# The engine that signals the entry of a kernel's main section: GpSimd in place of SyncE

## The chip, the cores and the metric

The kernel runs on one core of a Trainium2 chip. The metric is the time on the device of one execution, in microseconds (us). The core has a matrix engine (TensorE, PE in the profile, with PEld for its weight loads), VectorE (DVE), ScalarE (ACT), GpSimd (POOL) and SyncE (SP). Each has a sequencer of its own that works through its own list of instructions; the engines meet only through semaphores. A sequencer's own work (waits, branches, DMA issues) is shown with a q behind the engine's name. The transfers issued by SyncE and ScalarE run on the same 16 DMA engines; in the profile, SyncE's are queue q1 and ScalarE's are queue q10.

## The reference

For each of 128 samples b, a matrix of 128 by 128 is picked from eight by the sample's subject, and its product with the sample is added to the sample:

```python
x: (128, 128, 1024) float32; itok_B_0_7: (128,) int32; L0_cond_weights: (8, 128, 128) float32
w = weights[subjects]
out = jnp.einsum('bct,bcd->bdt', x, w)
x = x + out
```

So 67.1 MB of x are read and 67.1 MB written, beside 0.5 MB of matrices.

## The kernel before

The 128 samples are worked on in 32 turns of four samples (two halves, h, of two samples each). `x_all` holds 12 slots of one turn each in the core's memory; the sum is formed in place, so that a slot is loaded, added to, stored from, and loaded again.

Nearly all of the kernel is one section, opened at L190 with `tc.tile_critical()`. Within it nothing is ordered for the author: each engine's list is written out by hand, with semaphores. The lists are these.

- SyncE: the load of the eight matrices (L192) into the last slot's room, the load of the subjects (L195), and then, in the loop of L247, a wait for `s_added` and a store for each turn (the first one at L251, the others through `transfer`, L67), in pairs of turns towards the end.
- ScalarE: the loads of x, four transfers a turn, 128 in all, through `transfer` (L67). From turn 12 on a turn waits until its slot has been stored; turn 11, whose slot holds the raw matrices at first, waits until they have been sorted (`s_sort`).
- VectorE: the zeros (L197), the sorting of the matrices (two transposes, L208 and L227, and copies, L230), the clamping of the subjects (L211 to L217), and then in a loop of 32 turns (L263) the sum of a half (L186) and the two matrices of the next (L165).
- GpSimd: four of the sorting copies (L230), then for each turn a wait until its loads have landed, which it passes on to TensorE as `s_ready` (L242 to L245).
- TensorE: six passes over zeros while nothing has arrived (L200), then in a loop (L268) eight matrix products a turn (L174), each half after `s_go` (its matrices are in place) and `s_ready`.

Ahead of the section the program opens with a barrier of all engines, in which GpSimd gathers the others and then releases them; in the profile it stands under L297 (GpSimd also writes four constants there). At the section's entry one engine, the signalling engine, raises a semaphore with a NOP, and every engine, itself included, waits for it on the branch that leads into the section. The NOP stands under L190, the branches under L306. Where the section ends, the signalling engine raises another semaphore, all five engines drain, the signalling engine gathers the five and raises a semaphore with a second NOP; these stand under L190 too.

Behind the section comes a second, short one (L272), in which ScalarE waits for the stores that are still under way, and the last store (L275), of 4 MB, which SyncE issues once the first section has ended. The program ends with the wait for that store and two barriers (L306).

Of the kernel before, what the change touches and what calls it, by code (L numbers as in the profile page):

```python
# [80 lines left out]
def kernel(  # L81
# [48 lines left out]
    def emptied(i):  # L130
        turns = i // SLOTS
        return DMA * (H * G + 1) * turns - (DMA * G if i >= SLOTS and i % SLOTS == 0 else 0)

    def load(engine, i, q):
        transfer(
            nc,
            engine,
            xs[i % SLOTS][:, q, :],
            x[i * H * G + q].rearrange("(a r) t -> a (r t)", r=ROWS),
        ).then_inc(s_head if i * H * G + q < G else s_slot[i % SLOTS], DMA)  # L140

    def store(i, n):
        at = i % SLOTS * H * G * T
        return transfer(
            nc,
            nc.sync,
            out[i * H * G : (i + n) * H * G].rearrange("g d t -> d g t"),
            x_all[:, at : at + n * H * G * T].rearrange(
                "d (o t) -> d o t", o=1 if i >= NT - WHOLE else n
            ),  # L150
        )

    def subjects_of(i):
        _, subject = nc.values_load_multi_w_load_instructions(
            index[0:1, i] if isinstance(i, slice) else index[0:1, bass.ds(i * (H * G), H * G)],
            engines=[mybir.EngineType.DVE],
            min_val=0,
            max_val=S - 1,
            skip_runtime_bounds_check_because="the index is clamped on the chip above",
        )  # L160
        return subject

    def place(h, subject):
        for q in range(h * G, (h + 1) * G):
            copy = nc.vector.tensor_copy(ws[q], w_all[:, bass.ds(subject[q], 1), :])  # L165
        copy.then_inc(s_go, 1)

    def multiply(slot, h):
        nc.tensor.wait_ge(s_go, 1).then_inc(s_go, -1)
        nc.tensor.wait_ge(s_ready, 1).then_inc(s_ready, -1)  # L170
        for q in range(h * G, (h + 1) * G):
            for t in range(0, T, N):
                at = slot * (H * G * T) + (q * T + t)
                mm = nc.tensor.matmul(  # L174
                    ps[h][:, q % G, t : t + N],
                    ws[q][:, 0, :],
                    x_all[:, bass.ds(at, N)],
                    start=True,
                    stop=True,
                )  # L180
        mm.then_inc(s_product, 1)

    def add(slot, h):
        mine = x_all[:, bass.ds(slot * (H * G * T) + h * G * T, G * T)]
        nc.vector.wait_ge(s_product, 1).then_inc(s_product, -1)  # L185
        nc.vector.tensor_tensor(  # L186
            mine, ps[h].rearrange("d g t -> d (g t)"), mine, ALU.add
        ).then_inc(s_added, 1)

    with tc.tile_critical():  # L190

        nc.sync.dma_start(  # L192
            w_raw, weights.rearrange("s (u j) d -> (s u) (j d)", j=S)
        ).then_inc(s_wall, DMA)
        nc.sync.dma_start(given, subjects.rearrange("(o b) -> o b", o=1)).then_inc(s_given, DMA)  # L195

        nc.vector.memset(zeros, 0.0).then_inc(s_zeros, 1)  # L197
        nc.tensor.wait_ge(s_zeros, 1)
        for _ in range(IDLE):
            nc.tensor.matmul(  # L200
                ps[P_SLOTS - 1][:, G - 1, :N], zeros[:, :D], zeros, start=True, stop=True
            )

        nc.vector.wait_ge(s_wall, DMA)
        nc.vector.transpose(  # L208
            w_mid.rearrange("p (e h w j) -> p j h e w", e=S, h=4, w=4), w_raw
        ).then_inc(s_sort, 1)  # L210
        nc.vector.memset(index[:, B:], 0).then_inc(s_index, 1)  # L211
        nc.vector.wait_ge(s_given, DMA)
        nc.vector.tensor_scalar(near, given, -S, S - 1, ALU.max, ALU.min).then_inc(s_index, 1)  # L213
        nc.vector.wait_ge(s_index, 2)
        nc.vector.tensor_scalar(wrap, near, 0, S, ALU.is_lt, ALU.mult).then_inc(s_index, 1)  # L215
        nc.vector.wait_ge(s_index, 3)
        nc.vector.tensor_tensor(index[:, :B], near, wrap, ALU.add).then_inc(s_index, 1)  # L217
        for i in range(NT):
            if i == SLOTS - 1:
                nc.scalar.wait_ge(s_sort, SORTED)  # L220
            if i >= SLOTS:
                nc.scalar.wait_ge(s_slot[i % SLOTS], emptied(i))
            for q in range(H * G):
                load(nc.scalar, i, q)

        nc.vector.wait_ge(s_sort, 1)
        nc.vector.transpose(w_late, w_mid).then_inc(s_sort, 1)  # L227

        def sort(engine, o, v):
            engine.tensor_copy(  # L230
                w_all[32 * v : 32 * (v + 1), 2 * o : 2 * (o + 1), :],
                w_late[32 * o : 32 * (o + 1)].rearrange("c (e v d) -> c v e d", v=4, d=D)[:, v],
            ).then_inc(s_sort, 1)

        nc.vector.wait_ge(s_sort, 2)
        nc.gpsimd.wait_ge(s_sort, 2)
        for o in range(4):
            for v in range(4):
                sort(nc.gpsimd if v == 3 else nc.vector, o, v)
        for i in range(NT):  # L240
            if i == 0:
                nc.gpsimd.wait_ge(s_head, DMA * G).then_inc(s_ready, 1)  # L242
                nc.gpsimd.wait_ge(s_slot[0], DMA * G).then_inc(s_ready, 1)
            else:
                nc.gpsimd.wait_ge(s_slot[i % SLOTS], emptied(i) + DMA * H * G).then_inc(s_ready, H)  # L245

        for i in [*range(NT - SLOTS), *range(NT - SLOTS, NT, PAIR)]:  # L247
            n = 1 if i < NT - SLOTS else PAIR
            nc.sync.wait_ge(s_added, (i + n + (BEHIND if EARLY <= i < NT - LAST else 0)) * H)
            if i == 0:  # L250
                nc.sync.dma_start(  # L251
                    out[: H * G].rearrange("g d t -> d g t"), xs[0]
                ).then_inc(s_slot[0], DMA)
            elif i + n < NT:
                store(i, n).then_inc(s_slot[i % SLOTS], DMA)


        nc.vector.wait_ge(s_index, 4)
        nc.vector.wait_ge(s_sort, SORTED)
        subject = subjects_of(slice(0, H * G))  # L260
        for h in range(H):
            place(h, subject)
        with nc.vector.Fori(0, NT) as turn:  # L263
            subject = subjects_of(turn + 1)
            for h in range(H):
                add(turn % SLOTS, h)
                place(h, subject)
        with nc.tensor.Fori(0, NT) as turn:  # L268
            for h in range(H):
                multiply(turn % SLOTS, h)  # L270
# [39 lines left out]
```

## Time and profile before

| | |
|---|---|
| median of 3 runs | 323.01 us (322.72, 323.01, 323.01) |
| profiled execution, time | 322.73 us |
| profiled execution, span from first to last instruction | 320.9 us |
| TensorE busy | 248.9 us (78%), 518 matmuls |
| VectorE busy | 172.6 us (54%), 216 instructions |
| GpSimd busy | 1.9 us (1%), 8 instructions |
| moved by DMA | 134.76 MB, 420 GB/s over the span |

The span is the profile's own time axis, and all moments are counted from its start. The time of an execution is 1.8 us longer than its span. An engine's busy time leaves out what only its sequencer does. In a row of the view by line, the three numbers are the shortest, median and longest duration in ns, and the next two are the first and the last start in us; an instruction is listed when any part of it lies in the stretch asked for.

### The profile page before, as it was taken

Reading aid. Unit: us, or ns where it says so; the run is one execution under the profiler, and the core shown is the slowest. Engines: PE = TensorE matmul, PEld = TensorE weight load, DVE = VectorE, ACT = ScalarE, POOL = GpSimd, SP = SyncE. Lnnn points to the kernel's source line nnn. Section 1 sums busy time; section 2 is a strip of 40 time slices with the busy share of each in tenths; the row PEclk is TensorE's granted clock in tenths of the full one; section 3 lists DMA queues with packets and bytes.
Section 4 is the critical chain, followed back from the end, with each engine's and each line's share of the span. In section 5 each row is a group of like instructions: output and inputs, shape, how many; then the busy total and the mean of one; then the engine's idle time right before and its main releaser. Section 6 shows DMA issues by size and latency. Waiting matters only on the chain. (4 is left out here: it accounts for less than half of the span.)

```text
span 320.9 us, 2386 instructions
## 1 busy us (share of the span) xinstructions
PE 248.9 (78%) x518; PEld 102.8 (32%) x518; DVE 172.6 (54%) x216; POOL 1.9 (1%) x8
## 2 busy tenths in 40 slices
PE   6199999999997699998498469988599957874000
PEld 2134444444433244443133224333244422331000
DVE  4636776777676167775435362675367745066000
POOL 0200000000000000000000000000000000000000
PEclk9679999999999599999789797999799989599555
DMA  7999999999999999999999999999999999999996
GB/s 294 425 425 412 426 423 432 429 423 425 425 425 425 425 424 425 425 429 425 429 435 431 427 427 429 425 425 425 425 425 425 425 425 425 427 427 455 429 445 274
DMA packets 10803, 134.76 MB, mean 420 GB/s; under 512 B 2481, under 2 KB 2482, under 8 KB 3122
## 3 DMA queue, kind: packets, MB, share of 16 engines
q1 hardware_dynamic: 4658, 67.64, 49.7%
q10 hardware_dynamic: 6144, 67.12, 49.6%
q14 instruction: 1, 0.01, 0.0%
HBM read 67.63 MB, written 67.11 MB: 420 GB/s over the span
## 5 line engine op out<-in xcount | busy, mean ns | idle before, releaser
L174 PE MATMUL ps<-x_all,w 128*128 x512 | 243.8, 635 | 42.0 <-PEq L170 34.3
L186 DVE TENSOR_TENSOR x_all<-ps,x_all 128x2048 f32 x64 | 146.7, 2292 | 117.3 <-DVEq L185 117.3
L174 PEld LDWEIGHTS ps<-x_all,w 128*128 128x128 f32 x512 | 100.9, 203 | 185.2 <-issue 184.6
L165 DVE COPY w<-w_all 128x128 f32 x132 | 23.2, 219 | 0.8 <-DVE w_all L230 0.8
L200 PE MATMUL ps<-zeros 128*128 128x512 f32 x6 | 5.2, 1033 | 1.7 <-DVE zeros L197 1.7
L230 DVE COPY w_all<-x_all 32x256 f32<-32x256 f32 x12 | 3.9, 326 | 0.4
L208 DVE STREAM_TRANSPOSE x_all<-x_all 128x1024 f32<-128x1024 f32 x1 | 2.0, 1992 | 3.1 <-DMA x_all<-in_L_cond_weights_dram 3.1
L200 PEld LDWEIGHTS ps<-zeros 128*128 128x128 f32 x6 | 1.8, 328 | 3.7 <-issue 2.1
L230 POOL COPY w_all<-x_all 32x256 f32<-32x256 f32 x4 | 1.7, 425 | 8.3 <-DVE x_all L227 8.1
L227 DVE STREAM_TRANSPOSE x_all<-x_all 128x1024 f32<-128x1024 f32 x1 | 1.2, 1225 | 0.0
L197 DVE MEMSET zeros<- 128x512 f32 x1 | 0.5, 485 | 1.0 <-SPq L190 1.0
L217 DVE CUSTOM_DVE_ANT_0 index<-near,wrap 1x256 uint16<-1x256 uint16 x1 | 0.3, 280 | 0.0
L215 DVE TENSOR_SCALAR wrap<-near 1x128 int32<-1x128 int32 x1 | 0.2, 215 | 0.0
L213 DVE TENSOR_SCALAR near<-given 1x128 int32<-1x128 int32 x1 | 0.2, 205 | 0.0
L297 POOL MEMSET const-bfloat16-1.0<- 128x1 bf16 x1 | 0.1, 100 | 0.0
L297 POOL MEMSET const-float32-0.0<- 128x1 f32 x1 | 0.1, 98 | 0.2 <-issue 0.2
L297 POOL MEMSET const-uint8-127<- 128x1 uint8 x1 | 0.1, 98 | 0.0
L297 POOL MEMSET const-float32-1.0<- 128x1 f32 x1 | 0.1, 97 | 0.0
L297 DVE BASE_LOAD x1 | 0.0, 21 | 0.1
L211 DVE MEMSET index<- 1x4 int32 x1 | 0.1, 62 | 0.0
## 6 DMA issues: line engine op xcount, KB each, us to landing
x_all<-in_x_dram ACTq DMA_DIRECT2D x128, 512.0 KB, 34.2
out_dram<-x_all SPq DMA_DIRECT2D x20, 2048.0 KB, 18.3
out_dram<-x_all SPq DMA_DIRECT2D x6, 4096.0 KB, 30.3
x_all<-in_L_cond_weights_dram SPq DMA_DIRECT2D x1, 512.0 KB, 3.7
given<-in_itok_B_dram SPq DMA_DIRECT2D x1, 0.5 KB
```

Source lines behind the costliest of these rows:

```text
L165: copy = nc.vector.tensor_copy(ws[q], w_all[:, bass.ds(subject[q], 1), :])
L174: mm = nc.tensor.matmul(ps[h][:, q % G, t : t + N], ws[q][:, 0, :], x_all[:, bass.ds(at, N)], start=True, stop=True,)
L186: nc.vector.tensor_tensor(mine, ps[h].rearrange("d g t -> d (g t)"), mine, ALU.add).then_inc(s_added, 1)
L197: nc.vector.memset(zeros, 0.0).then_inc(s_zeros, 1)
L200: nc.tensor.matmul(ps[P_SLOTS - 1][:, G - 1, :N], zeros[:, :D], zeros, start=True, stop=True)
L208: nc.vector.transpose(w_mid.rearrange("p (e h w j) -> p j h e w", e=S, h=4, w=4), w_raw).then_inc(s_sort, 1)
L213: nc.vector.tensor_scalar(near, given, -S, S - 1, ALU.max, ALU.min).then_inc(s_index, 1)
L215: nc.vector.tensor_scalar(wrap, near, 0, S, ALU.is_lt, ALU.mult).then_inc(s_index, 1)
L217: nc.vector.tensor_tensor(index[:, :B], near, wrap, ALU.add).then_inc(s_index, 1)
L227: nc.vector.transpose(w_late, w_mid).then_inc(s_sort, 1)
L230: engine.tensor_copy(w_all[32 * v : 32 * (v + 1), 2 * o : 2 * (o + 1), :], w_late[32 * o : 32 * (o + 1)].rearrange("c (e v d) -> c v e d", ...
L297: nc = _bacc.Bacc("TRN2", target_bir_lowering=False, num_devices=1)
```

## The change

One argument is added. It names the engine that signals the entry and the end of the main section. Without it that engine is SyncE here.

```diff
-    with tc.tile_critical():
+    with tc.tile_critical(sync_engine=mybir.EngineType.Pool):
 
         nc.sync.dma_start(
             w_raw, weights.rearrange("s (u j) d -> (s u) (j d)", j=S)
```

No transfer, compute instruction, wait or size of the section itself is changed; the second section, at L272, keeps ScalarE as its signalling engine.

## The prediction

> **What bounds the kernel now.** I read the page first: the table of slices, the DMA queues, the total traffic.
>
> ```profile
> span 320.9 us, 2386 instructions
> ...
> DMA  7999999999999999999999999999999999999996
> ...
> q1 hardware_dynamic: 4658, 67.64, 49.7%
> q10 hardware_dynamic: 6144, 67.12, 49.6%
> ...
> HBM read 67.63 MB, written 67.11 MB: 420 GB/s over the span
> ```
>
> Only the first and last of 40 DMA slices are under 9, and both queues together fill 99.3% of the 16 engines. So I asked for the stretches at the two ends and between them (start:end us, length, four engines, granted clock, DMA share, GB/s).
>
> ```profile
> 1.50:2.01 0.51, 0.34 (x1) 0.34 (x2) 0.11 (x1) 0.00 (x0) 1.00 0.00 0
> 2.01:2.03 0.02, 0.02 (x1) 0.02 (x1) 0.00 (x0) 0.00 (x0) 1.00 6.40 410
> 2.03:6.00 3.97, 3.97 (x5) 1.48 (x5) 1.29 (x1) 0.00 (x0) 1.00 0.98 369
> 6.00:300.00 294.00, 244.60 (x514) 100.94 (x512) 170.82 (x214) 1.70 (x4) 0.92 1.01 427
> 300.00:317.50 17.50, 0.00 (x0) 0.00 (x0) 0.00 (x0) 0.00 (x0) 0.50 0.98 419
> ...
> 318.40:320.00 1.60, 0.00 (x0) 0.00 (x0) 0.00 (x0) 0.00 (x0) 0.50 0.01 0
> ```
>
> No byte starts before 2.01 us, none after 318.4, and between 6 and 300 us the engines move 427 GB/s at a share of 1.01. 134.76 MB (the page's two directions added) at 427 GB/s take 315.6 us; the stream stands from 2.01 to about 318.3. What can be won is at the ends: 2.0 us ahead of the first byte, about 2.6 us behind the last, and 1.8 us outside the span (the profiled execution took 322.73 us). PE and DVE may move by tenths without an effect as long as both queues are supplied. The end of the span is a wait for the last store, in the DMA queues' own waits:
>
> ```profile
> SPq L306 <- DMA out_dram<-x_all: 23.7, 1, 23.7
> ```
>
> Now the first two microseconds, in order of time:
>
> ```profile
> 0.34 0.10 POOL L297 MEMSET const-uint8-127<- 128x1 uint8 x1
> 0.90 1.18 ACTq L67 DMA_DIRECT2D x_all<-in_x_dram  x2
> 0.96 0.41 SPq L192 DMA_DIRECT2D x_all<-in_L_cond_weights_dram  x1
> 1.12 0.48 DVE L197 MEMSET zeros<- 128x512 f32 x1 [0.99 <-SPq L190]
> ```
>
> DVE's first work of the section is put down to SP's line 190, the entry of the section: this is the signal that the change takes from SyncE. The sequencers' own instructions appear in the view by line; one-decimal starts are too coarse, so I asked for stretches of hundredths. The rows below come from 0.605:0.615, 0.645:0.665 (two rows), 0.71:0.72, 0.75:0.765 (two rows) and 0.79:0.82 us:
>
> ```profile
> L297 POOLq EVENT_SEMAPHORE  x1: 17/17/17, 0.6 to 0.6; - x1
> ...
> L297 SPq EVENT_SEMAPHORE  x1: 17/17/17, 0.7 to 0.7; - x1
> L297 ACTq EVENT_SEMAPHORE  x1: 17/17/17, 0.7 to 0.7; - x1
> ...
> L190 SPq NOP  x1: 18/18/18, 0.7 to 0.7; - x1
> ...
> L306 ACTq COMPARE_BRANCH  x1: 33/33/33, 0.8 to 0.8; - x1
> L306 POOLq COMPARE_BRANCH  x1: 33/33/33, 0.8 to 0.8; - x1
> ...
> L306 SPq COMPARE_BRANCH  x1: 33/33/33, 0.8 to 0.8; - x1
> ```
>
> This is a ladder of two signals. GpSimd ends the program's opening barrier at 0.61 and the others see it at 0.655: a hop of 0.045. SyncE goes on to its NOP at 0.715 (0.06 after its event), which is the entry signal; ScalarE and GpSimd branch into the section at 0.757 (a hop of 0.042). SyncE, which has to pass its own NOP, branches only at 0.80. The first DMA issues follow, ScalarE's at 0.90 and SyncE's at 0.96: 0.14 to 0.16 behind their branches.
>
> **The change, part by part.** *Entry.* The NOP and its signal move from SyncE to GpSimd; no transfer and no compute instruction is added or removed. GpSimd raises the barrier itself, so it need not see it first: the SyncE hop goes. No row shows a NOP on GpSimd; I give it SyncE's step from barrier to NOP, 0.06, so it falls at 0.61 + 0.06 = 0.67, and a hop of 0.042 brings it to the others at 0.71. ScalarE and SyncE are themselves ready at 0.655 + 0.06 = 0.715; that is late next, so nothing better can come. ScalarE's branch moves from 0.757 to 0.715: -0.04. SyncE's moves from 0.80 to 0.715: -0.08. Behind the new wait on SyncE stand the loads of the matrices (L192) and of the subjects (L195); on ScalarE the loads of x; on DVE the zeros.
>
> Which of the two queues opens the stream? From 2.00 to 3.76 us the DMA view answers:
>
> ```profile
> DMA packets 108, 0.44 MB, mean 251 GB/s; under 512 B 0, under 2 KB 0, under 8 KB 108
> ...
> q1 hardware_dynamic: 108, 0.44, 86.7%
> ```
>
> Queue 1 alone, in small packets: the matrices, issued by SyncE. x, though issued 0.06 us earlier, has no packet before 3.76. So the start of the stream goes with SyncE's issue, and I take -0.08; if it went with ScalarE's it would be -0.04. The best end is -0.08. The worst uses the longest GpSimd sequencer row of the page's end that waits for nothing:
>
> ```profile
> L306 POOLq EVENT_SEMAPHORE_RANGE_CLEAR  x1: 201/201/201, 320.4 to 320.4; - x1
> ```
>
> A NOP that took 0.20 would signal at 0.87, seen at 0.91: +0.11 on SyncE and +0.15 on ScalarE. I stay near SyncE's NOP because GpSimd's EVENT_SEMAPHORE (17 ns) and COMPARE_BRANCH (33 ns) above take exactly what ScalarE's take.
>
> [...]
>
> *What the earlier start does.* The stream is full from 6 us on, so a start 0.08 earlier ends 0.08 earlier. Matrices that land 0.08 earlier let the sort and the first product start 0.08 earlier; that is worth nothing more, as DMA and not PE is full.
>
> *Exit.* The end of the section is signalled by the same engine, so it moves to GpSimd too. Now (295 to 296 us, then the closing wait of ScalarE, and GpSimd's waits for x):
>
> ```profile
> L190 SPq EVENT_SEMAPHORE  x3: 17/28/28, 295.3 to 295.5; - x3
> ...
> L190 POOLq DRAIN  x1: 41/41/41, 295.3 to 295.3; - x1
> L190 DVEq DRAIN  x1: 85/85/85, 295.3 to 295.3; - x1
> ...
> L190 SPq NOP  x1: 13/13/13, 295.6 to 295.6; - x1
> ...
> L306 ACTq EVENT_SEMAPHORE  x5: 38/38/14502, 295.7 to 310.5; - x5
> ...
> L245 POOLq EVENT_SEMAPHORE  x31: 17/17/17, 14.6 to 285.1; - x31
> ```
>
> SyncE signals the end, five engines drain, SyncE gathers them and goes on in its own program to the last store. With GpSimd gathering, the last store waits for one more hop, +0.04, and its gather may cost up to the 0.20 above. GpSimd is there in time: its last wait ends at 285.1, ten microseconds ahead. The cost is hidden: from 295.7 to the end the queue moves this much,
>
> ```profile
> q1 hardware_dynamic: 343, 9.67, 93.3%
> ...
> out_dram<-x_all SPq DMA_DIRECT2D x1, 4096.0 KB, 24.3
> ```
>
> of which 4.19 MB are the last store. The other 5.48 MB are stores queued ahead of it, 13 us at 419 GB/s, and ScalarE sees the last of those land only 14.5 us after 295.7. So 0.24 us of delay costs nothing; without that cover it would cost 0.24. Behind the last store SyncE has only the final wait.
>
> Sum: 322.73 - 0.08 (entry) + 0 (exit, hidden) = 322.65 for the profiled execution. That execution lies 0.28 below the median of the runs shown, 323.01, whose lowest is 322.72; from the median the forecast is 323.01 - 0.08 = **322.93**. A difference of 0.2% (0.65 us) is about what a measurement of this kernel can tell from no change, and 0.08 is an eighth of it: **no change that can be measured**.
>
> **The rivals.** *Nothing is gained, or GpSimd's NOP is slow.* If the NOP on GpSimd takes effect no earlier than 0.715, the start stays: 322.73, or 323.01 from the median. If it takes 0.20, the start slips by 0.11: 322.84, or 323.12. For it: no GpSimd NOP is in the trace. Also within 0.2%.
>
> *Slower: the engines' last packets.* The stream's end is uneven. In 318.23:318.40, and then in 318.35:319.30, the DMA view has
>
> ```profile
> q1 hardware_dynamic: 3, 0.10, 135.4%
> ...
> q1 hardware_dynamic: 13, 0.00, 0.8%
> ```
>
> Three last packets of 33 KB start when the other 13 engines are already finishing (13 packets without bytes). At 427/16 = 26.7 GB/s per engine one packet takes 1.23 us. If the shifted start changes how loads and stores alternate so that one engine falls a further packet behind, the end slips by 1.23: 322.65 + 1.23 = 323.88 (324.16 from the median), slower by 0.36%. It decides from half a packet on (0.65 us). Against it: every engine has the same bytes to move, and three runs of one program differ by only 0.29 us.
>
> *Faster: the same place, evened out.* The 0.10 MB spread over 16 engines take 0.23 us instead of 1.23: at best 1.0 us less, 321.65 (321.93). The same argument stands against it, and nothing in the change aims there.
>
> *Slower: x passes the matrices.* If x's first transfers reached the engines ahead of the matrices, each would delay them by 0.524 MB / 427 GB/s = 1.23 us, and sort, products and stores with them. The time grows only once the loads of the 12 slots (25.2 MB, 59 us at that rate, from 3.76 to 63) are through before the first store (the rows below: issued at 26.9, landed 23.8 later, at 50.7) has emptied a slot. That is 12 us of delay, or ten transfers passed; each further one costs 1.23: 322.65 + 1.23 = 323.88 for one. Against it: SyncE gains 0.04 on ScalarE by the change.
>
> ```profile
> L251 SPq DMA_DIRECT2D out_dram<-x_all x1: 424/424/424, 26.9 to 26.9; - x1
> ...
> DMA to landing us min/median/max: 23.8/23.8/23.8
> ```
>
> **How the numbers follow.** Forecast (entry 0.04 to 0.08 earlier) 0.70; nothing gained or a slow NOP 0.15; an engine a packet later 0.07; evened out 0.06; x ahead 0.02. The first two stay within 0.2%: same 0.85; slower 0.09; faster 0.06. The time is 322.93. The range takes the first two cases, which hold 0.85: from 322.93 less the runs' spread of 0.29, and 0.14 for a part of the even tail, 322.50; to 323.12 and, for a part of a later packet, 0.23: 323.35.
>
> **What would show it.** DVE's wait at L197 names GpSimd's queue at line 190, and the NOP of line 190 stands on GpSimd at 0.67. ScalarE's first issue is at 0.86 and SyncE's at 0.88; the first byte at 1.93 to 1.97; queue 1 alone until x starts at 3.7. The last store's issue stays within 0.2 us of 295.7 and its end at 318.2 to 319.6. I am wrong if the first byte comes later than 2.13, if DMA falls under 425 GB/s between 6 and 300 us, or if more or fewer than three packets are late at the end.

## The result, and the profile after

The changed kernel takes 323.73 us (median of 12 runs, 323.42 to 324.47), the kernel before 323.02 (12 runs, 322.72 to 323.61). The ratio is 1.0020, with a 95% interval of 1.0011 to 1.0029: slower by 0.7 us, where 322.93 and no measurable change were forecast. The range ended at 323.35.

The page of the changed kernel hardly differs, and the stretches (start:end, length, the four engines, granted clock, DMA share, GB/s) show the stream as full as before:

```profile
span 321.5 us, 2387 instructions
...
q1 hardware_dynamic: 4658, 67.64, 49.8%
q10 hardware_dynamic: 6144, 67.12, 49.5%
...
HBM read 67.63 MB, written 67.11 MB: 419 GB/s over the span
```

```profile
1.50:1.92 0.42, 0.25 (x1) 0.25 (x2) 0.11 (x1) 0.00 (x0) 1.00 0.00 0
1.92:1.94 0.02, 0.02 (x1) 0.02 (x2) 0.00 (x0) 0.00 (x0) 1.00 3.04 205
...
6.00:300.00 294.00, 239.93 (x513) 99.30 (x512) 170.97 (x214) 1.70 (x4) 0.93 1.01 427
300.00:317.50 17.50, 0.00 (x0) 0.00 (x0) 0.00 (x0) 0.00 (x0) 0.50 0.98 419
```

The rate between 6 and 300 us is the same 427 GB/s, and the first byte comes at 1.92 to 1.94 instead of 2.01 to 2.03: 0.09 earlier, close to the 0.08 that was forecast. The entry itself, first the order of time, then the view by line in stretches of hundredths (0.685:0.70, 0.725:0.735, 0.74:0.75 us):

```profile
0.89 1.18 ACTq L67 DMA_DIRECT2D x_all<-in_x_dram  x2
0.89 0.41 SPq L192 DMA_DIRECT2D x_all<-in_L_cond_weights_dram  x1
1.13 0.48 DVE L197 MEMSET zeros<- 128x512 f32 x1 [0.99 <-PEq L297]
```

```profile
L190 POOLq NOP  x1: 13/13/13, 0.7 to 0.7; - x1
...
L306 SPq COMPARE_BRANCH  x1: 33/33/33, 0.7 to 0.7; - x1
...
L306 ACTq COMPARE_BRANCH  x1: 33/33/33, 0.7 to 0.7; - x1
```

GpSimd's NOP stands at 0.69 and takes 13 ns. SyncE branches at 0.73 (0.80 before), ScalarE at 0.74 (0.757 before); their first issues now fall together.

So where are the 0.7 us? The profiled execution has a span of 321.5 and a time of 323.96: 2.46 us lie outside the span. Before it was 322.73 - 320.9 = 1.83. This holds for every run: the time less the span is 2.34 to 2.62 in the twelve runs of the changed kernel (median 2.47), and 1.73 to 1.84 in 132 runs of the kernel before that were made beside the experiments (median 1.78). The spans do not differ: on the mean 321.29 and 321.31. **All of the 0.7 us lies outside the span.** There, from 321 to 325 us (40 slices of 0.1 us), the DMA view of the changed kernel has one packet:

```profile
DMA  0000000000000000000000000000200000000000
GB/s 0 0 0 0 0 0 0 0 0 0 0 0 0 0 0 0 0 0 0 0 0 0 0 0 0 0 0 0 82 0 0 0 0 0 0 0 0 0 0 0
DMA packets 1, 0.01 MB, mean 2 GB/s; under 512 B 0, under 2 KB 0, under 8 KB 0
...
q14 instruction: 1, 0.01, 0.6%
```

and the same stretch of the kernel before has none:

```profile
DMA packets 0, 0.00 MB, mean 0 GB/s; under 512 B 0, under 2 KB 0, under 8 KB 0
```

It is a packet of instructions (82 GB/s for 0.1 us: 8.2 KB), at 323.8, which is 2.3 us behind the end of the span. My reading is that an engine fetches more of its list there; the view does not say which engine. The page does not tell the kernels apart in this: its count for q14 is 1 in both, for a packet that both profiles have between 116 and 117 us. The change moves instructions from one list to another: in the two programs GpSimd's list grows from 60 to 65 instructions, SyncE's shrinks from 49 to 45, the others stay. (The profiled executions agree in the differences: they hold 55 and 60 instructions of GpSimd, 45 and 41 of SyncE.)

### The profile page after: what moved, and what is told of

Its sections match the earlier page's. It is cut to its first block, busy times and chain, and to the rows that moved or that the text cites. A ratio compares the mean times of both kernels' runs of the same rounds, so it can differ in the third digit from the quotient of the medians.

```text
span 321.5 us, 2387 instructions
## 1 busy us (share of the span) xinstructions
PE 244.3 (76%) x518; PEld 101.1 (31%) x518; DVE 172.6 (54%) x216; POOL 1.9 (1%) x8
## 5 line engine op out<-in xcount | busy, mean ns | idle before, releaser
L174 PE MATMUL ps<-x_all,w 128*128 x512 | 239.6, 626 | 44.8 <-PEq L170 30.5
L174 PEld LDWEIGHTS ps<-x_all,w 128*128 128x128 f32 x512 | 99.3, 199 | 185.1 <-issue 184.5
L197 DVE MEMSET zeros<- 128x512 f32 x1 | 0.5, 485 | 1.0 <-PEq L297 1.0
L297 POOL MEMSET const-bfloat16-1.0<- 128x1 bf16 x1 | 0.1, 101 | 0.0
L297 POOL MEMSET const-float32-0.0<- 128x1 f32 x1 | 0.1, 98 | 0.2 <-issue 0.2
L297 POOL MEMSET const-float32-1.0<- 128x1 f32 x1 | 0.1, 98 | 0.0
L297 POOL MEMSET const-uint8-127<- 128x1 uint8 x1 | 0.1, 98 | 0.0
```

The source lines that it names most:

```text
L174: mm = nc.tensor.matmul(ps[h][:, q % G, t : t + N], ws[q][:, 0, :], x_all[:, bass.ds(at, N)], start=True, stop=True,)
L297: nc = _bacc.Bacc("TRN2", target_bir_lowering=False, num_devices=1)
```

## The experiments

Theory "outside": the price is the fetch, and hangs on the length of GpSimd's list. Rival "start": the two first issues now fall together, which lays the stream out worse. A later rival says that the cost comes of GpSimd's signalling, whatever the length of its list. `s_spare` in the edits is a semaphore that nobody waits for. Each kernel ran eleven times beside the kernel before; "outside" is the median of time less span.

**The kernel before again** (no edit).

> The kernel before, unchanged: it measures how far two equal programs differ, and how much of a time lies outside the span (the profiled execution before: 322.73 - 320.9 = 1.83 us; the changed kernel: 323.96 - 321.5 = 2.46, and 2.34 to 2.62 in all twelve of its executions). Theory 'outside the span' (the change costs its 0.6 us there): about 1.8 us outside, 323.0. Theory 'start' (the first issues of SyncE and ScalarE now fall together and the stream is laid out worse): nothing said of the outside; 323.0 and a span of 320.9 to 321.2. If about 2.4 us lies outside here too, the theory of the outside is dead.

Measured: 323.02, ratio 0.9998 (0.9989 to 1.0007), outside 1.78. Equal programs agree within the interval, and the outside belongs to the program.

**The changed kernel with SyncE's first issue later.**

```diff
     with tc.tile_critical(sync_engine=mybir.EngineType.Pool):
+        nc.sync.sem_inc(s_spare, 1)
         nc.sync.dma_start(
```

> The changed kernel with one semaphore increment more on SyncE ahead of the load of the matrices, some 0.06 to 0.08 us, which puts SyncE's first issue behind ScalarE's again (0.89 and 0.96 instead of 0.891 and 0.892). Theory 'start': back to 323.0, 0.7 under the changed kernel. Theory 'outside the span': stays at 323.7, as GpSimd still signals.

Measured: 323.79, ratio 1.0022 (1.0013 to 1.0031), outside 2.52. The issues are apart again, at 0.89 and 0.99:

```profile
0.89 0.53 ACTq L67 DMA_DIRECT2D x_all<-in_x_dram  x1
0.99 0.41 SPq L192 DMA_DIRECT2D x_all<-in_L_cond_weights_dram  x1
```

and nothing of the 0.7 us comes back. This speaks against "start".

**The kernel before with ScalarE's first issue later.**

```diff
+        nc.scalar.sem_inc(s_spare, 1)
...
         for i in range(NT):
             if i == SLOTS - 1:
```

> The kernel before with one semaphore increment more on ScalarE ahead of the loads of x, some 0.06 to 0.08 us, so that ScalarE's first issue falls together with SyncE's (0.97 and 0.96) while SyncE still signals. Theory 'start': 323.7, as slow as the changed kernel. Theory 'outside the span': 323.0.

Measured: 323.04, ratio 0.9999 (0.9990 to 1.0008), outside 1.79. The issues come within 0.02 of each other, at 0.95 and 0.97, and nothing is lost:

```profile
0.95 0.41 SPq L192 DMA_DIRECT2D x_all<-in_L_cond_weights_dram  x1
0.97 0.53 ACTq L67 DMA_DIRECT2D x_all<-in_x_dram  x1
```

Neither run bears "start" out, and the equal spans above speak against it too.

**The kernel before with GpSimd's list as long as in the changed kernel.**

```diff
                 nc.gpsimd.wait_ge(s_slot[i % SLOTS], emptied(i) + DMA * H * G).then_inc(s_ready, H)
+        nc.gpsimd.sem_inc(s_spare, 1); nc.gpsimd.sem_inc(s_spare, 1); nc.gpsimd.sem_inc(s_spare, 1); nc.gpsimd.sem_inc(s_spare, 1); nc.gpsimd.sem_inc(s_spare, 1)
```

> The kernel before with five semaphore increments more at the end of GpSimd's list in the section, which is then as long as in the changed kernel; they run at about 285 us, when nobody waits for GpSimd. Theory 'outside the span', if it is the length of GpSimd's list: 323.7 with 2.4 us outside the span. Theory 'start': 323.0.

Measured: 323.81, ratio 1.0020 (1.0011 to 1.0029), outside 2.52. SyncE signals, as before; five instructions that nobody waits for bring the whole loss, and the packet at the same place, 2.3 us behind a span of 321.1:

```profile
core 0 of [0], span 321.1 us
DMA  0000000000000000000000003000000000000000
...
DMA packets 1, 0.01 MB, mean 2 GB/s; under 512 B 0, under 2 KB 0, under 8 KB 0
...
q14 instruction: 1, 0.01, 0.8%
```

**Two instructions instead of five** (62).

```diff
+        nc.gpsimd.sem_inc(s_spare, 1); nc.gpsimd.sem_inc(s_spare, 1)
```

> The kernel before with two more semaphore increments at the end of GpSimd's list in the section (60 instructions become 62; 65 in the changed kernel). Theory 'a block of the list is fetched behind the span': the cost comes in one step of about 0.7 us at some length between 60 and 65, so either 323.0 with 1.78 us outside the span and no packet of instructions there, or 323.75 with 2.5 us and one packet. Rival 'each instruction on GpSimd costs': a part in proportion, 2/5 of 0.75 = 0.3, so 323.35.

Measured: 322.93, ratio 1.0001 (0.9992 to 1.0010), outside 1.80, no packet. So it is not a price per instruction.

**Another engine's list:** five increments on VectorE behind its loop (VectorE's list grows from 62 to 68).

```diff
                 place(h, subject)
+        for _ in range(5): nc.vector.sem_inc(s_spare, 1)
         with nc.tensor.Fori(0, NT) as turn:
```

> The kernel before with five more semaphore increments on VectorE behind its loop (and one register instruction that comes with them: 62 become 68, more than the 65 of GpSimd in the changed kernel). If any engine's list costs a fetch past some length, 323.75 with 2.5 us outside the span; if it is GpSimd's own matter, 323.0 and 1.78. The span itself stays at 321.3 by either, as the last store is far behind.

Measured: 323.11, ratio 1.0003 (0.9994 to 1.0012), outside 1.81. Neither branch of the expectation: there is a packet, but it costs 0.03. It comes earlier, in the slice at 322.3, 1.1 to 1.2 us behind the span of 321.2:

```profile
DMA  0000000000000200000000000000000000000000
```

**GpSimd's four sorting copies on VectorE**, in the changed kernel and, as control, in the kernel before (GpSimd 61 and 56, VectorE 66 in both).

```diff
-        nc.gpsimd.wait_ge(s_sort, 2)
...
-                sort(nc.gpsimd if v == 3 else nc.vector, o, v)
+                sort(nc.vector, o, v)
```

> The changed kernel, GpSimd still signals, but GpSimd's four sorting copies run on VectorE, which brings GpSimd's list down from 65 to 61 instructions and VectorE's up from 62 to 66. Theory 'the length of GpSimd's list': if the step lies above 61, 323.0 or a few hundredths less, 1.78 us outside the span, no packet of instructions behind it. Rival 'that GpSimd signals costs, whatever its length': 323.75 and 2.5. The sort is 1.3 us longer on VectorE, which the full DMA queues hide.

> The control for the run above: the kernel before, SyncE signals, with the four sorting copies on VectorE (GpSimd's list 56, VectorE's 66). By each theory 323.0, with 1.78 us outside the span and a span of 321.3; a difference from that is the price of the moved copies and is to be taken off the run above.

Measured: 323.34, ratio 1.0008 (0.9999 to 1.0017), outside 2.21; control 323.48, ratio 1.0017 (1.0008 to 1.0026), outside 2.19. The control, which should have cost nothing, costs as much: both profiles have a packet 1.7 us behind the span, and some 0.42 us more lie outside, whoever signals. I read it as a fetch of VectorE's longer list. Once that is taken off, GpSimd's signal costs nothing at 61; but the pair was a poor way to ask, as it moved two lists.

**The changed kernel with a shorter list**, nothing moved elsewhere (61).

```diff
+            elif i in (1, 3, 5, 7):
+                nc.gpsimd.wait_ge(s_slot[i], DMA * H * G)
             else:
-                nc.gpsimd.wait_ge(s_slot[i % SLOTS], emptied(i) + DMA * H * G).then_inc(s_ready, H)
+                nc.gpsimd.wait_ge(s_slot[i % SLOTS], emptied(i) + DMA * H * G).then_inc(s_ready, 2 * H if i in (2, 4, 6, 8) else H)
```

> The changed kernel, GpSimd signals, with GpSimd's list in the section cut from 65 to 61 instructions: turns 1 and 2, 3 and 4, 5 and 6, 7 and 8 are reported to TensorE by one instruction for two turns each; nothing moves to another engine. Theory 'the length of GpSimd's list': no packet of instructions behind the span, 1.78 us outside it, 323.0, or 322.95 if the entry's few hundredths show. Rival 'that GpSimd signals costs': 323.75, 2.5 us outside.

Measured: 322.92, ratio 0.9995 (0.9986 to 1.0004), outside 1.78, no packet. GpSimd signals, the two issues stand together at 0.89 as in the changed kernel, and the 0.7 us are gone:

```profile
core 0 of [0], span 321.2 us
...
DMA packets 0, 0.00 MB, mean 0 GB/s; under 512 B 0, under 2 KB 0, under 8 KB 0
```

This undoes the loss without undoing the change. It is no measurable gain over the kernel before.

**Four more on the kernel before (64), four and twelve more on the changed kernel (69 and 77)**: the same line, at the same place, with four, four and twelve increments.

> The kernel before with four more semaphore increments at the end of GpSimd's list (64 instructions; 62 cost nothing, 65 cost 0.7 us). Theory 'a block is fetched': one of the two levels, 323.0 with 1.78 us outside and no packet, or 323.75 with 2.5 us and one packet; nothing between.

> The changed kernel with four more semaphore increments on GpSimd (69 instructions instead of 65). Theory 'where the fetch falls sets its price': a longer list meets the end of its block earlier; VectorE's four more instructions put the fetch at 1.68 us behind the span for 0.42 us, two more still put it at 1.18 for 0.04. So here the fetch comes earlier than the 2.29 us of the changed kernel and costs less, 0.1 to 0.5: 2.0 to 2.3 us outside, 323.1 to 323.5. Rival 'a fetch costs 0.7, or more instructions cost more': 323.75 or above.

> The changed kernel with twelve more semaphore increments on GpSimd (77 instructions instead of 65). Theory 'where the fetch falls sets its price': the fetch comes earlier than 1.3 us behind the span, where GpSimd still has time before it is waited for: 0.0 to 0.1, so 1.78 to 1.9 us outside and 323.05, although the list is longer than in the changed kernel. Rival 'a fetch costs 0.7, or more instructions cost more': 323.75 or above.

Measured: 64: 323.29, ratio 1.0005 (0.9996 to 1.0014), outside 2.05, no packet in the profile. 69: 323.39, ratio 1.0006 (0.9997 to 1.0015), outside 2.06 in the median, but 1.74 and 1.75 in two of the eleven, of which the profiled one is one, without a packet. 77: 323.25, ratio 1.0010 (1.0001 to 1.0019), outside 1.79. The value of 64 lies between the two levels, where nothing was expected. 77 is as expected outside the span: the list is the longest and nothing is lost there. Its packet comes in the slice at 321.6, 0.1 to 0.2 us behind the span of 321.5:

```profile
DMA  0000003000000000000000000000000000000000
```

Its span, however, was 321.56 on the mean, against 321.32 beside it; 73 (321.25) does not share that, so it does not come of the length alone, and it stays open.

**Lengths 63, 67, 71 and 73 in the changed kernel**: two, six and eight increments in the same line, and for 63 only two pairs of turns.

```diff
+            elif i in (1, 3):
+                nc.gpsimd.wait_ge(s_slot[i], DMA * H * G)
...
+                nc.gpsimd.wait_ge(s_slot[i % SLOTS], emptied(i) + DMA * H * G).then_inc(s_ready, 2 * H if i in (2, 4) else H)
```

> The changed kernel with GpSimd's list cut from 65 to 63 instructions (turns 1 and 2, and 3 and 4, reported by one instruction each). Lengths of 61 and 62 cost nothing, 64 cost 0.27 us without a packet of instructions in its profile, 65 cost 0.7. Theory 'the length decides, in steps': 0 or 0.27, so 1.78 or 2.05 us outside the span. Rival 'the price of 64 belongs to the four added increments and not to the length': 0, 1.78, while nothing between 0 and 0.7 appears in this series.

> The changed kernel with two more semaphore increments on GpSimd (67 instructions). Theory 'the price is a saw in the length': between 65 (2.5 us outside) and 69 (2.06) it lies in between or on one of the two, 2.06 to 2.5. Rival 'only the step counts, 69 was a chance': 2.5.

> The changed kernel with six more semaphore increments on GpSimd (71 instructions). Theory 'the price is a saw in the length': the fetch is on its way forward to where 77 has it (0.19 us behind the span), 1.8 to 2.2 us outside. Rival 'only the step counts': 2.5.

> The changed kernel with eight more semaphore increments on GpSimd (73 instructions). Theory 'the price is a saw in the length': fetch within the first microsecond behind the span, 1.78 to 1.9 us outside, 323.0 to 323.2. Rival 'only the step counts': 2.5. The span of 77 was 0.25 us longer than before (321.56 against 321.32, means of 11 and 33); if that comes of the length, this span is longer too.

Measured: 63: 323.01, ratio 0.9999 (0.9990 to 1.0008), outside 1.81. 67: 323.03, ratio 0.9997 (0.9988 to 1.0006), outside 1.78. 71: 323.41, ratio 1.0009 (1.0000 to 1.0018), outside 2.02. 73: 323.44, ratio 1.0013 (1.0004 to 1.0022), outside 2.26. 67 and 73 miss: 67 costs nothing where 0.3 to 0.7 was expected, 73 costs 0.48 outside where at most 0.1 was. 73 has its packet 0.9 to 1.0 us behind its span of 321.3:

```profile
DMA  0000000000003000000000000000000000000000
```

All lengths of GpSimd's list together, whoever signals, from the kernels that leave VectorE's list at 62:

| instructions | outside, us | packet recorded, us behind the span |
|---|---|---|
| 60, 61, 62, 63 | 1.78, 1.78, 1.80, 1.81 | none |
| 64 | 2.05 | none |
| 65 (three kernels) | 2.47, 2.52, 2.52 | 2.3 |
| 67 | 1.78 | none |
| 69 | 2.06 (1.74 and 1.75 in 2 of 11) | none |
| 71 | 2.02 | 1.6 |
| 73 | 2.26 | 0.9 to 1.0 |
| 77 | 1.79 | 0.1 to 0.2 |

Shown: the length of the list decides whether time is lost, not the signal; the price is not one step, and 67 and 77 are free again. Argued, not shown: that the fetch is what takes the time, and that a list is fetched block by block, as some of the expectations assume; the views show single packets of 8.2 KB in the instruction queue and name no engine. A packet goes with the loss at 65, 71 and 73, but 64 costs 0.27, and 0.24 in its profiled execution, without a recorded packet, and 77 has a packet and costs nothing. At 69 the profiled execution is one of the two that lost nothing, so its missing packet says nothing of the other nine. It is also open why 67 is free; the saw that I expected would have fallen evenly.

## Why the prediction was wrong

**The bound** was right: 427 GB/s between 6 and 300 us in both, and only the ends could change.

**The entry** was right to a few hundredths. GpSimd's NOP was put at 0.67 and stands at 0.69; SyncE's issue was put at 0.88 and stands at 0.89. ScalarE gained less than was put: its first issue stands at 0.89 instead of 0.86, as its branch came at 0.74 and not at 0.715. The slow NOP (0.20) of the second case did not come: it took 13 ns, where SyncE's had taken 18. One sign that I named was a bad one: DVE's wait at L197 is put down to PEq L297 and not to GpSimd, since a releaser is inferred from whatever came last; the L190 row is what shows the change.

**Its worth** was mis-sized: -0.08 was carried through the full stream to the end, and the spans do not show it. They are 321.30 on the mean of 111 runs of the ten kernels in which GpSimd signals, 321.31 in 132 runs of the kernel before, 321.29 in 66 runs of six others in which SyncE does. With a standard error of 0.02 to 0.03 each, a gain of 0.08 should just have appeared. Without the kernel of 77, whose span was longer than the others', the others come to 321.27, so that a part of the gain cannot be excluded. Where the rest goes is open: in this profile the matrices land later although they start earlier,

```profile
x_all<-in_L_cond_weights_dram SPq DMA_DIRECT2D x1, 512.0 KB, 4.0
```

4.0 us after the issue instead of 3.7; but from one profile to another of these kernels that number goes from 3.5 to 4.2, whoever signals.

**The exit** had the wrong sign. The last store does not wait for GpSimd's gathering: SyncE's own wait for the last sum is enough. The last sum of the kernel before and that of the changed one, rows of 290 to 296 us of the changed one, and its line of the stores:

```profile
292.81 2.29 DVE L186 TENSOR_TENSOR x_all<-ps,x_all 128x2048 f32 x1 [0.81 <-DVEq L185]
...
290.94 2.29 DVE L186 TENSOR_TENSOR x_all<-ps,x_all 128x2048 f32 x1 [0.81 <-DVEq L185]
...
L190 POOLq EVENT_SEMAPHORE  x2: 43/43/43, 293.6 to 293.7; - x2
...
L190 POOLq NOP  x1: 13/13/13, 293.8 to 293.8; - x1
...
L67 SPq DMA_DIRECT2D out_dram<-x_all x25: 538/539/12876, 33.6 to 293.5; - x25
```

The store is issued at 293.5, 0.3 ahead of GpSimd's NOP and 0.3 behind the end of the last sum (293.2); before, it was issued at 295.7, 0.6 behind that sum's end (295.1). So some 0.3 of the 2.2 us come of the gathering, the rest of a last sum that ended earlier in this profile. The sign that the issue stays within 0.2 us of 295.7 thus failed. The earlier issue is hidden behind the stores queued ahead, as was argued (ScalarE's wait for them takes 16.9 us from 293.9 on), and the spans show no gain from it.

**The step that failed** is the sum itself: "322.73 - 0.08 (entry) + 0 (exit, hidden)". It carries the 1.8 us outside the span over unchanged, and they became 2.47. I had written that "no transfer and no compute instruction is added or removed", and looked at the moved instructions where they run. That they lengthen GpSimd's list by five, at entry and exit, and what a longer list does behind the span, was no term of the sum and no rival. The missing term measures 0.7 us, and the run with five idle increments in the kernel before gives it alone. The loss is also clear of the noise: 0.2% was taken as about the least that can be told, but with twelve runs each the interval is 0.09% to either side.

**The rivals.** "The engines' last packets" would have given the right sign for a wrong reason; in this very profile something still moves in the last stretch,

```profile
318.40:320.00 1.60, 0.00 (x0) 0.00 (x0) 0.00 (x0) 0.00 (x0) 0.50 0.05 21
```

1.6 us at 21 GB/s, or 33 KB, one packet that starts after 318.4 where before none did; and its span is 0.6 longer. So the signs on the stream's end (three late packets, an end by 319.6) were missed in this profile. The twelve runs refute it as the cause: on the mean their spans equal those of before. x did not pass the matrices; from 2.0 to 3.7 us queue 1 still moves alone:

```profile
DMA packets 90, 0.37 MB, mean 217 GB/s; under 512 B 0, under 2 KB 0, under 8 KB 90
...
q1 hardware_dynamic: 90, 0.37, 81.0%
```

## What to carry to other kernels

A change of one argument can lengthen an engine's instruction list (GpSimd's from 60 to 65 here); count the lists before and after, and do not take the time outside the span for a constant (1.78 and 2.47 us here). When two kernels differ by as little as these, 0.2%, subtract the span from the time in every run first: it told in one step, here, that neither the entry nor the stream was to blame. And test such a suspicion by adding idle instructions to the old kernel, not by more readings of the new one.

## What the runs showed of the hardware that was not expected

A packet of some 8.2 KB of instructions can move after the last instruction of the span. With it 0.69 us more lay outside the span where it came 2.3 us behind the span (list of GpSimd, 65 instructions), 0.42 at 1.7 (VectorE, 66), 0.24 at 1.6 (GpSimd, 71), 0.03 at 1.1 to 1.2 (VectorE, 68), but 0.48 at 0.9 to 1.0 (GpSimd, 73), and nothing at 0.1 to 0.2 (GpSimd, 77). So the place alone does not set the price. And a kernel can get faster by instructions that do nothing: the changed kernel with two more of them (67) ran at 323.03, against 323.73 without.
